# The LayerNorm's Newton step of the first stage from VectorE to GpSimd, and its normalised rows one row block per step

## The chip, the cores and the metric

The kernel runs on one core of a Trainium2 chip. The metric is the device time of one execution in microseconds; runs of one kernel are compared by their median. The profile is that of one profiled execution on the same core. PE is TensorE, DVE is VectorE, ACT is ScalarE, POOL is GpSimd, and SP is the engine whose queue issues most of the transfers.

## The reference

One decoder layer on x of shape (2, 2048, 512), that is 4096 rows of 512, in float32: a fixed-weight attention block, a cross attention over 128 context rows, and a mixture of 32 experts with a shared expert. The change touches the first block only:

```python
def _layernorm(x, axis=-1, eps=1e-05):
    m = jnp.mean(x, axis=axis, keepdims=True)
    v = jnp.var(x, axis=axis, keepdims=True)
    return (x - m) / jnp.sqrt(v + eps)

def attn(residual):                    # residual = _layernorm(x)
    x = _layernorm_gb(residual, ln_g, ln_b)   # the same again, with gain and bias
    q = x.reshape(Bx, Tx, 4, 128).transpose(0, 2, 1, 3)
    k = w_fc.reshape(-1, 128)          # 2048 keys
    v = w_proj.T.reshape(-1, 128)
    p = jnp.square(jax.nn.relu(jnp.einsum('bhtd,sd->bhts', q, k)))
    out = jnp.einsum('bhts,sd->bhtd', p, v)
    return residual + merged_heads(out)

x = x + attn(_layernorm(x))            # first stage
x = x + cross_attention(_layernorm(x), ctx, mask)
x = x + mixture_of_experts(_layernorm(x))
```

Both LayerNorms in a row need two reciprocal square roots of the same variance: with v the variance of a row, 1/sqrt(v + eps) for the residual, and 1/sqrt(v(1 + eps) + eps^2), the two in one, for the rows that go into the attention. The kernel computes them together as eight columns for the four row blocks of a tile.

## The kernel before

The work is one program of four parts: the first stage (`stage0`), the cross attention (`stage1`), the shared expert with the routing (`shared`), and the experts (`routed`). All matrix products are split: a float32 operand is written as a high and a low part (`split`, L89 to L97: the high part by a cast on ACT or DVE, the low part by a subtraction on DVE or POOL), and three matmuls make one product.

`stage0` handles 8 tiles of 512 rows. Its main loop runs over `steps`, (tile t, head h, key block kt): 8 x 4 x 16 = 512 steps. A step makes one 128x512 score tile `s` with three matmuls (L349) in one of four PSUM banks (P1 and P2, two each, by the parity of kt), lets ACT take the relu `rl` (L353) and DVE multiply `s` by it (L357, the square), splits the result into `ph` and `pl` (for five steps of eight, those with the result in SBUF, `pl` is made by POOL, for the other three by DVE), and multiplies `ph`, `pl` with the values (`av`, L311) seven steps later (LAG = 7).

Between these steps the next tile is prepared by the generator `prep(t + 1)`: at kt = 2 of head 0 it loads four row blocks `xt` (L238), and from kt = 7 on every odd kt calls it once. A call makes one part up to the next `yield`:

- four times `bn_stats` and `bn_aggr` of a row block on DVE (L243, L244), one call each
- `ve` (L247, L248) on DVE, the power -0.5 on POOL (`power`, L249, into `ap`), and on DVE one Newton step of it (L250 to L252: `at`, `at`, `ar`) and the offsets `ao` = -mean * `ar` (L254)
- the normalised rows `y` of the four row blocks on ACT (L264), two per call
- `bv` = 1 + `ar` on DVE (L270), and on POOL the residual rows x + layernorm(x), in place in `xt` (L273), each stored to `x1` by SP (L274), two per call

Tile 0 is prepared ahead of the loop, with two of its rows made by DVE. `prep_head` (L278) later turns the rows `y` by transposes on PE (L281), applies gain and bias on ACT (`gb`, L282) and splits them into `qh` and `ql`. Another generator, `background`, does context and weight work in other steps (wk, wv, wq, wo, and the shared expert's sums); its loads and stores go through SP's queue too.

The order within each engine's queue isn't the program's order. A scheduler places the instructions by their priority and by a simulated timeline when the kernel is built. The queues then run in that order on the chip, each waiting on semaphores. The same pools of tiles are shared by all: `xt` has four buffers, `y` six.

Of the kernel before, what the change touches and what calls it, by code (L numbers as in the profile page):

```python
# [14 lines left out]
A = mybir.AluOpType  # L15
# [65 lines left out]
@contextmanager  # L81
def later(g, n):

    g.tc.cur_priority += n
    yield
    g.tc.cur_priority -= n


def split(g, hi, lo, src, lo_engine=None, hi_engine=None):  # L89

    if isinstance(lo_engine, cycle):
        lo_engine = next(lo_engine)
    if hi_engine is None:
        g.nc.scalar.copy(hi, src)  # L94
    else:
        hi_engine.tensor_copy(hi, src)
    g.low = (lo_engine or g.nc.vector).tensor_tensor(lo, src, f32(hi), A.subtract)  # L97
# [16 lines left out]
def weight_steps(g, dram, nk, width, name, lo_engine=None):  # L114
    hi, lo = ([[g.piece(name + z)[:] for _ in range(width // 512)] for _ in range(nk)] for z in "hl")
    yield from split_steps(g, dram, hi, lo, lo_engine)
    return hi, lo


def part(w, k, c):  # L120

    return w[k][c // 4][:, c % 4 * 128:c % 4 * 128 + 128]


def run(steps):

    try:
        while True:
            next(steps)
    except StopIteration as end:  # L130
        return end.value
# [31 lines left out]
def three(terms):  # L163

    (wh, wl), (xh, xl) = terms
    return (wl, xh), (wh, xl), (wh, xh)
# [55 lines left out]
def stage0(g, x, wfcT, wpT, lnT, x1, background, front):  # L222
    nc = g.nc
    NT = T // 512
    LAG = 7
    gb = g.c.tile([128, 2, 4], F32, name="gb")
    with later(g, 20):
        nc.sync.dma_start(gb[:], lnT)
    ys, qs = {}, {}

    def prep(t):

        rows = [slice(t * 512 + s * 128, t * 512 + s * 128 + 128) for s in range(4)]
        xt = [g.tile("G", "xt") for _ in rows]
        for v, r in zip(xt, rows):
            nc.sync.dma_start(v[:], x[r, :])  # L238
        yield
        mv = g.sm.tile([128, 4, 2], F32, name="am", tag="am")  # L240
        for i, v in enumerate(xt):
            s6 = g.small("as", 6)
            nc.vector.bn_stats(s6[:], v[:])  # L243
            nc.vector.bn_aggr(mv[:, i, :], s6[:])  # L244
            yield
        ve, r0, tt, rs, of = (g.small("a" + z, 8) for z in "vptro")
        nc.vector.tensor_scalar(ve[:, 0:4], mv[:, :, 1], EPS, None, A.add)  # L247
        nc.vector.tensor_scalar(ve[:, 4:8], mv[:, :, 1], 1.0 + EPS, EPS * EPS, A.mult, A.add)  # L248
        power = nc.gpsimd.tensor_tensor(r0[:], ve[:], g.mhalf[:], A.pow)  # L249
        nc.vector.scalar_tensor_tensor(tt[:], r0[:], -0.5, ve[:], A.mult, A.mult)  # L250
        nc.vector.tensor_tensor(tt[:], tt[:], r0[:], A.mult)
        nc.vector.scalar_tensor_tensor(rs[:], tt[:], 1.5, r0[:], A.add, A.mult)  # L252
        mean = mv[:, :, 0].unsqueeze(1).to_broadcast([128, 2, 4])
        nc.vector.scalar_tensor_tensor(of[:].rearrange("p (a n) -> p a n", a=2), mean, -1.0,  # L254
                                       rs[:].rearrange("p (a n) -> p a n", a=2), A.mult, A.mult)
        if t > 0:
            yield
        ys[t] = []
        for i, v in enumerate(xt):
            y = g.tile("C", "y")  # L260
            if t == 0 and i % 2:
                g.first = nc.vector.tensor_scalar(y[:], v[:], mv[:, i, 0:1], rs[:, 4 + i:5 + i], A.subtract, A.mult)
            else:
                nc.scalar.activation(y[:], v[:], AF.Identity, bias=of[:, 4 + i:5 + i], scale=rs[:, 4 + i:5 + i])  # L264
            ys[t].append(y)
            if i % 2:
                yield

        sc = g.small("bv", 4)
        nc.vector.tensor_scalar(sc[:], rs[:, 0:4], 1.0, None, A.add)  # L270
        for i, v in enumerate(xt):
            with g.after(power):
                nc.gpsimd.tensor_scalar(v[:], v[:], sc[:, i:i + 1], of[:, i:i + 1], A.mult, A.add)  # L273
            nc.sync.dma_start(x1[rows[i], :], v[:])  # L274
            if i % 2:
                yield

    def prep_head(t, h):  # L278
        pt = g.bank("P4", "pt")
        for s in range(4):  # L280
            nc.tensor.transpose(pt[:, s * 128:(s + 1) * 128], ys[t][s][:, h * 128:(h + 1) * 128], g.ident)  # L281
        g.q = nc.scalar.activation(pt[:], pt[:], AF.Identity, bias=gb[:, 1, h:h + 1], scale=gb[:, 0, h:h + 1])  # L282
        qh, ql = g.tile("E", "qh", FR), g.tile("F", "ql", FR)
        split(g, qh[:], ql[:], pt[:])
        qs[t, h] = (qh, ql)

    todo = prep(0)
    while 0 not in ys or len(ys[0]) < 4:
        next(todo)
    with g.after(g.first):  # L290
        kw = run(weight_steps(g, wfcT, 4, 512, "kw", cycle((nc.vector, nc.gpsimd))))
    low = g.low
    prep_head(0, 0)
    prep_head(0, 1)
    with g.after(g.q):
        vw = run(weight_steps(g, wpT, 4, 512, "vw"))
    with g.after(low):
        run(todo)
    prep_head(0, 2)
    prep_head(0, 3)  # L300

    P, oT, cur = {}, {}, {}

    def av(t, h, kt):
        p = P.pop((t, h, kt))
        if kt == 0:
            cur["o"] = g.bank("P3", "o")
        o = cur["o"]
        j, rb = divmod(kt, 4)
        for n, (w, y) in enumerate(three(([part(v, rb, j) for v in vw], p))):  # L310
            nc.tensor.matmul(o[:], w, y[:], start=kt == 0 and n == 0, stop=kt == 15 and n == 2)  # L311
        if kt < 15:
            return
        oT[h] = g.tile("D", "oT")
        nc.scalar.copy(oT[h][:], o[:])
        if h < 3:
            return
        for s in range(4):
            rows = x1[t * 512 + s * 128:t * 512 + s * 128 + 128, :]
            b = g.tile("IJ"[s % 2] if t < NT - 1 else "G", "b")  # L320
            nc.sync.dma_start(b[:], rows)
            pt = g.bank("P4", "pt")
            for hh in range(4):
                nc.tensor.transpose(pt[:, hh * 128:(hh + 1) * 128], oT[hh][:, s * 128:(s + 1) * 128], g.ident)
            nc.vector.tensor_tensor(b[:], pt[:], b[:], A.add)
            nc.sync.dma_start(rows, b[:])

    steps = [(t, h, kt) for t in range(NT) for h in range(4) for kt in range(16)]
    marks = []
    for i, (t, h, kt) in enumerate(steps):  # L330
        if h == 0 and kt == 2 and t + 1 < NT:
            todo = prep(t + 1)
            next(todo)
        if t + 1 == NT and h == 0 and kt == 14:
            todo = front
        if (t + 1 < NT and (h > 0 or kt > 6) or h > 0) and kt % 2:
            with g.after(*marks):
                next(todo, None)
        if (h > 0 if t > 0 else h > 1) and kt % 8 == 6 or t > 0 and h == 0 and kt == 14:
            with g.after(*marks):  # L340
                next(background, None)
        if h > 0 and t + 1 < NT and kt == 12:
            prep_head(t + 1, h - 1)
        if h == 0 and t > 0 and kt == 8:
            prep_head(t, 3)
        s = g.bank(("P1", "P2")[kt % 2], "s")
        j, rb = divmod(kt, 4)
        for n, (w, y) in enumerate(three(([part(k, j, rb) for k in kw], qs[t, h]))):
            nc.tensor.matmul(s[:], w, y[:], start=n == 0, stop=n == 2)  # L349
        if i >= LAG:  # L350
            av(*steps[i - LAG])
        r = g.tile("K", "rl")
        m0 = nc.scalar.activation(r[:], s[:], AF.Relu)  # L353

        apart = i % 8 in (1, 3, 5, 6, 7)
        p = g.tile("H", "p") if apart else s
        m1 = nc.vector.tensor_tensor(p[:], s[:], r[:], A.mult)  # L357
        marks = [m0, m1]
        ph, pl = g.tile("A", "ph", FR), g.tile("B", "pl", FR)
        split(g, ph[:], pl[:], p[:], nc.gpsimd if apart else None, nc.vector if i % 8 == 2 else None)  # L360
        P[t, h, kt] = (ph, pl)
    run(background)
    g.marks = marks
    for st in steps[len(steps) - LAG:]:
        av(*st)
# [1219 lines left out]
```

## Time and profile before

| | us |
|---|---|
| median of 3 runs | 2690.44 (2690.38 to 2690.57) |
| profiled execution | 2688.47 |
| its span, first to last instruction | 2686.7 |
| PE busy | 2631.5 (98%) |
| DVE busy | 2047.4 (76%) |
| ACT busy | 1873.9 (70%) |
| POOL busy | 1208.4 (45%) |
| mean granted TensorE clock | 0.997 |
| x1, the residual rows on POOL (L273) | 32 of 0.835 mean |
| the power on POOL (L249) | 8 of 1.646 mean |

The first column of a timeline row is the start in us from the span's start, the second the duration in us; then come the engine, the line, the operation, out<-in by the program's names, the shapes, the number of merged instructions, and in brackets the idle time of the engine just before and what released it. A row of a group has the number of instructions, the total busy us and the mean ns of one, and the idle time before them with its releasers. Line numbers are those of the kernel before.

### The profile page before, as it was taken

Reading aid. Unit: us, or ns where it says so; the run is one execution under the profiler, and the core shown is the slowest. Engines: PE = TensorE matmul, PEld = TensorE weight load, DVE = VectorE, ACT = ScalarE, POOL = GpSimd, SP = SyncE. Lnnn points to the kernel's source line nnn. Section 1 sums busy time; section 2 is a strip of 40 time slices with the busy share of each in tenths; the row PEclk is TensorE's granted clock in tenths of the full one; section 3 lists DMA queues with packets and bytes.
Section 4 is the critical chain, followed back from the end, with each engine's and each line's share of the span. In section 5 each row is a group of like instructions: output and inputs, shape, how many; then the busy total and the mean of one; then the engine's idle time right before and its main releaser. Section 6 shows DMA issues by size and latency. Waiting matters only on the chain. (4 is left out here: it accounts for less than half of the span.)

```text
span 2686.7 us, 47611 instructions
## 1 busy us (share of the span) xinstructions
PE 2631.5 (98%) x14593; PEld 2265.3 (84%) x14593; DVE 2047.4 (76%) x4569; ACT 1873.9 (70%) x4155; POOL 1208.4 (45%) x972
## 2 busy tenths in 40 slices
PE   7999999999999999999999999999999999999998
PEld 5888877877789999999988877878989899888886
DVE  7777777777777888898876794663777777778985
ACT  7887787788778778887874332343666677777885
POOL 5765676777654444444446569420122212212221
PEclk9999999999999999999999999999999999999999
DMA  4112112223120323433259656663898899999994
GB/s 154 60 67 95 56 60 91 93 104 102 41 75 23 103 97 127 130 128 131 88 183 358 213 188 203 237 224 94 266 283 280 280 306 294 303 280 292 330 323 139
DMA packets 282289, 463.72 MB, mean 173 GB/s; under 512 B 34512, under 2 KB 85712, under 8 KB 282032
## 3 DMA queue, kind: packets, MB, share of 16 engines
q1 hardware_dynamic: 267344, 433.50, 47.3%
q0 software_dynamic: 14688, 27.17, 4.8%
q8 instruction: 115, 1.88, 0.3%
q14 instruction: 142, 1.16, 0.1%
HBM read 359.58 MB, written 102.93 MB: 172 GB/s over the span
## 5 line engine op out<-in xcount | busy, mean ns | idle before, releaser
L97 DVE TENSOR_TENSOR rl<-raw,rh 128x512 fp32r<-128x512 f32 x768 | 488.0, 684 | 82.5 <-ACT rh L94 63.1
L94 ACT CAST rh<-raw 128x512 fp32r<-128x512 f32 x768 | 438.7, 621 | 130.0 <-DMA raw<-in_rg 87.2
L97 POOL TENSOR_TENSOR pl<-p,ph 128x512 fp32r<-128x512 f32 x320 | 411.1, 1297 | 232.8 <-ACT ph L94 199.2
L353 ACT ACTIVATE rl<-s 128x512 f32<-128x512 f32 x512 | 294.1, 605 | 43.3 <-PE s L349 36.5
L1356 POOL DMA_INDIRECT out_dram<-v,idx x46 | 112.8, 2452 | 462.1 <-ACT v L1354 377.9
L526 POOL TENSOR_TENSOR e<-e,ri 128x512 f32<-128x512 f32 x128 | 134.0, 1052 | 289.8 <-DVE ri L524 145.3
L357 DVE TENSOR_TENSOR p<-s,rl 128x512 f32<-128x512 f32 x320 | 215.2, 683 | 45.2 <-ACT rl L353 38.8
L94 ACT CAST ph<-p 128x512 fp32r<-128x512 f32 x320 | 199.9, 629 | 53.3 <-DVE p L357 51.3
L523 ACT ACTIVATE e<-e,mn 128x128 f32<-128x128 f32 x512 | 199.7, 392 | 25.1 <-DVE mn L518 23.7
L349 PE MATMUL s<-qh,kwl 128*128 128x512 f32 x512 | 206.1, 404 | 10.0 <-DVE p L357 6.4
L1019 PE MATMUL gu<-z,swh 128*128 128x512 f32 x672 | 209.5, 391 | 0.2 <-DMA z<-zT 0.2
L357 DVE TENSOR_TENSOR s<-s,rl 128x512 f32<-128x512 f32 x192 | 133.5, 695 | 98.4 <-ACT rl L353 97.9
L311 PE MATMUL o<-pl,vwh 128*128 128x512 f32 x512 | 203.1, 397 | 1.2 <-POOL pl L97 1.2
L311 PE MATMUL o<-ph,vwl 128*128 128x512 f32 x512 | 200.4, 393 | 0.7 <-ACT ph L94 0.7
L349 PE MATMUL s<-ql,kwh 128*128 128x512 f32 x512 | 200.1, 391 | 0.0
L349 PE MATMUL s<-qh,kwh 128*128 128x512 f32 x512 | 200.0, 391 | 0.0
L311 PE MATMUL o<-ph,vwh 128*128 128x512 f32 x512 | 199.7, 390 | 0.0
L496 PE MATMUL q<-yh,wql 128*128 128x256 f32 x512 | 147.3, 288 | 2.1 <-DVE v L556 2.1
L1019 PEld LDWEIGHTS gu<-z,swh 128*128 128x128 f32 x672 | 126.3, 188 | 26.5 <-DMA z<-zT 0.6
L496 PE MATMUL q<-yh,wqh 128*128 128x256 f32 x512 | 146.1, 285 | 0.0
L496 PE MATMUL q<-yl,wqh 128*128 128x256 f32 x512 | 145.9, 285 | 0.0
L97 DVE TENSOR_TENSOR pl<-s,ph 128x512 fp32r<-128x512 f32 x192 | 131.3, 684 | 16.9 <-ACT ph L94 13.9
(348 smaller groups left out, 7986.0 us busy)
## 6 DMA issues: line engine op xcount, KB each, us to landing
raw<-in_rg SPq DMA_DIRECT2D x256, 256.0 KB
raw<-in_ru SPq DMA_DIRECT2D x256, 256.0 KB
raw<-in_rd SPq DMA_DIRECT2D x256, 256.0 KB
z<-zT SPq DMA_DIRECT2D x112, 256.0 KB
raw<-in_sgu SPq DMA_DIRECT2D x48, 256.0 KB
swh<-wS SPq DMA_DIRECT2D x48, 256.0 KB
swl<-wS SPq DMA_DIRECT2D x48, 256.0 KB
xt<-in_x SPq DMA_DIRECT2D x32, 256.0 KB
```

The costliest lines, as they stand in the source:

```text
L94: g.nc.scalar.copy(hi, src)
L97: g.low = (lo_engine or g.nc.vector).tensor_tensor(lo, src, f32(hi), A.subtract)
L311: nc.tensor.matmul(o[:], w, y[:], start=kt == 0 and n == 0, stop=kt == 15 and n == 2)
L349: nc.tensor.matmul(s[:], w, y[:], start=n == 0, stop=n == 2)
L353: m0 = nc.scalar.activation(r[:], s[:], AF.Relu)
L357: m1 = nc.vector.tensor_tensor(p[:], s[:], r[:], A.mult)
L496: nc.tensor.matmul(o[:, i, :], part(w, k, p), y[k // 2][:, k % 2, :], start=n == 0, stop=n == 11)
L523: nc.scalar.activation(e[:, hs], e[:, hs], AF.Exp, bias=mn[:, h:h + 1], scale=-1.0, accum_out=su[:, h:h + 1])
L526: nc.gpsimd.tensor_tensor(e4, e4, ri[:].unsqueeze(2).to_broadcast([128, 4, 128]), A.mult)
L1019: nc.tensor.matmul(o[:], y, z, start=(at, x) not in begun, stop=j == 1 and m == 2, skip_group_check=True)
L1356: nc.gpsimd.indirect_dma_start(out=out, out_offset=bass.IndirectOffsetOnAxis(ap=idx[rows, b + j:b + j + 1], axis=0), in_=v[rows], in_offse ...
```

## The change

From tile 1 on, the Newton step, the offsets and `bv` are made by POOL instead of DVE. The five operations are written as eight: two products, a scaling with an addition, a product, two products for the offsets and their sign, and the addition for `bv`. One more `yield` stands behind them, and the normalised rows come one per call instead of two. Tile 0 stays as it was.

```diff
@@ prep(t) in stage0
         power = nc.gpsimd.tensor_tensor(r0[:], ve[:], g.mhalf[:], A.pow)
-        nc.vector.scalar_tensor_tensor(tt[:], r0[:], -0.5, ve[:], A.mult, A.mult)
-        nc.vector.tensor_tensor(tt[:], tt[:], r0[:], A.mult)
-        nc.vector.scalar_tensor_tensor(rs[:], tt[:], 1.5, r0[:], A.add, A.mult)
-        mean = mv[:, :, 0].unsqueeze(1).to_broadcast([128, 2, 4])
-        nc.vector.scalar_tensor_tensor(of[:].rearrange("p (a n) -> p a n", a=2), mean, -1.0,
-                                       rs[:].rearrange("p (a n) -> p a n", a=2), A.mult, A.mult)
-        if t > 0:
+        V = nc.vector if t == 0 else nc.gpsimd
+        if t == 0:
...
+        else:
+            V.tensor_tensor(tt[:], r0[:], r0[:], A.mult)
+            V.tensor_tensor(tt[:], tt[:], ve[:], A.mult)
+            V.tensor_scalar(tt[:], tt[:], -0.5, 1.5, A.mult, A.add)
+            V.tensor_tensor(rs[:], tt[:], r0[:], A.mult)
+            for a in range(2):
+                V.tensor_tensor(of[:, 4 * a:4 * a + 4], mv[:, :, 0], rs[:, 4 * a:4 * a + 4], A.mult)
+            V.tensor_scalar(of[:], of[:], -1.0, None, A.mult)
+            yield
             yield
         ys[t] = []
         for i, v in enumerate(xt):
...
             ys[t].append(y)
-            if i % 2:
+            if i % 2 or t > 0:
                 yield
 
         sc = g.small("bv", 4)
-        nc.vector.tensor_scalar(sc[:], rs[:, 0:4], 1.0, None, A.add)
+        V.tensor_scalar(sc[:], rs[:, 0:4], 1.0, None, A.add)
         for i, v in enumerate(xt):
```

In the changed kernel the lines from L250 on stand up to ten lines later: the new operations are L259 to L265, `bv` is L280, the rows `y` L274, the residual rows L283, the relu L363, the square L367.

More of the change, by code (lines that the diff above doesn't have):

```diff
@@ L249, in prep @@
         power = nc.gpsimd.tensor_tensor(r0[:], ve[:], g.mhalf[:], A.pow)
-        nc.vector.scalar_tensor_tensor(tt[:], r0[:], -0.5, ve[:], A.mult, A.mult)
-        nc.vector.tensor_tensor(tt[:], tt[:], r0[:], A.mult)
-        nc.vector.scalar_tensor_tensor(rs[:], tt[:], 1.5, r0[:], A.add, A.mult)
-        mean = mv[:, :, 0].unsqueeze(1).to_broadcast([128, 2, 4])
-        nc.vector.scalar_tensor_tensor(of[:].rearrange("p (a n) -> p a n", a=2), mean, -1.0,
-                                       rs[:].rearrange("p (a n) -> p a n", a=2), A.mult, A.mult)
-        if t > 0:
+        V = nc.vector if t == 0 else nc.gpsimd
+        if t == 0:
+            V.scalar_tensor_tensor(tt[:], r0[:], -0.5, ve[:], A.mult, A.mult)
+            V.tensor_tensor(tt[:], tt[:], r0[:], A.mult)
+            V.scalar_tensor_tensor(rs[:], tt[:], 1.5, r0[:], A.add, A.mult)
+            mean = mv[:, :, 0].unsqueeze(1).to_broadcast([128, 2, 4])
+            V.scalar_tensor_tensor(of[:].rearrange("p (a n) -> p a n", a=2), mean, -1.0,
+                                   rs[:].rearrange("p (a n) -> p a n", a=2), A.mult, A.mult)
+        else:
[7 more added lines that the diff above has]
+            yield
             yield
```

## The prediction

> **What bounds the kernel now.** I read the page first, then PE's timeline in the first stage, then DVE, ACT and POOL at the places where PE pauses, last the groups by form.
>
> ```profile
> span 2686.7 us, 47611 instructions
> PE 2631.5 (98%) x14593; PEld 2265.3 (84%) x14593; DVE 2047.4 (76%) x4569; ACT 1873.9 (70%) x4155; POOL 1208.4 (45%) x972
> ```
>
> PE is the bound. The first stage is a stream of 128x512 matmuls whose starts are 0.227 us apart, six per step (1.36 us). Only what interrupts that stream can be won. I went through PE's timeline from 40 to 690 us and added up what lies over 0.227 between one start and the next where it is over by 0.09 or more. All of it sits in seven places, at the preparations of tiles 1 to 7 (tile 0 is prepared before the loop): 2.8, 1.7, 1.7, 2.5, 2.5, 3.5 and 2.6 us, 17.3 in all. Between them no start is late by that much. So 17.3 us is the most that this change can bring. The largest pause of tile 4, on PE:
>
> ```profile
> 345.68 0.50 PE L311 MATMUL o<-ph,vwl 128*128 128x512 f32 x1
> 347.64 0.50 PE L349 MATMUL s<-qh,kwl 128*128 128x512 f32 x1 [1.46 <-DVE p L357]
> ```
>
> A score matmul waits for its bank, which DVE's squaring (L357) frees. Why DVE was late is seen on tile 3, in the timelines of POOL, DVE and ACT:
>
> ```profile
> 236.64 1.65 POOL L249 TENSOR_TENSOR ap<-av,mhalf 128x8 f32<-128x8 f32 x1 [1.58 <-DVE av L248]
> 238.26 2.55 POOL L97 TENSOR_TENSOR pl<-p,ph 128x512 fp32r<-128x512 f32 x2
> ...
> 238.33 1.25 DVE L250 SCALAR_TENSOR_TENSOR at<-ap,av 128x8 f32<-128x8 f32 x1 [0.84 <-POOL ap L249]
> 239.61 0.70 DVE L357 TENSOR_TENSOR s<-s,rl 128x512 f32<-128x512 f32 x1
> 240.22 0.61 DVE L251 TENSOR_TENSOR at<-at,ap 128x8 f32<-128x8 f32 x1
> ...
> 240.34 0.59 ACT L94 CAST ph<-s 128x512 fp32r<-128x512 f32 x1 [1.42 <-DVE s L357]
> ...
> 242.53 2.92 ACT L264 ACTIVATE y<-xt,ao,ar 128x512 f32<-128x512 f32 x4
> ```
>
> Three costs stand there. DVE, whose queue is in order, stops 0.84 us for the power. Its 128x8 operation then takes 1.25 us and ends as the first of POOL's two subtractions ends (238.26 + 1.3): a tiny operation on DVE waits for whatever POOL is running. And ACT does four normalised rows in one piece of 2.9 us, in which no score tile gets its relu. The groups (window 40 to 690) give the second cost its size:
>
> ```profile
> L270 DVE TENSOR_SCALAR bv<-ar 128x4 f32<-128x4 f32 x7 | 7.3, 1048 | 0.0
> L250 DVE SCALAR_TENSOR_TENSOR at<-ap,av 128x8 f32<-128x8 f32 x7 | 6.1, 865 | 2.1 <-POOL ap L249 2.0
> L251 DVE TENSOR_TENSOR at<-at,ap 128x8 f32<-128x8 f32 x7 | 5.5, 779 | 0.0
> L252 DVE SCALAR_TENSOR_TENSOR ar<-at,ap 128x8 f32<-128x8 f32 x7 | 3.8, 539 | 0.0
> L254 DVE SCALAR_TENSOR_TENSOR ao<-am,ar 128x8 f32<-128x8 f32 x7 | 1.1, 154 | 0.0
> ```
>
> In tile 0, where POOL is idle, the same five took 0.15 to 0.17 us each.
>
> **Removed.** Seven times five operations leave DVE: 7.3 + 6.1 + 5.5 + 3.8 + 1.1 = 23.8 us, and the 2.1 us of waiting for the power. DVE is busy 76%, so this is worth nothing by itself; it is worth the PE pauses that it causes. ACT's wait for ao in front of the rows (L264 idle 3.2 us in this stage, two tiles) goes as well, unless the new ao is late. Only the two additions and scalings that give ve (L247, L248) stay on DVE.
>
> **Added.** Eight operations per tile on POOL, 56 in all. No row has a 128x8 product on POOL. Bounds: 0.105 us (the MEMSET of mhalf, 128x8) and 0.70 us (the power on 128x2, L139). The nearest rows by kind are the subtractions on 128x256 (0.742) and 128x512 (1.297); the line through them gives 0.20 at 8 columns. Dependent ones follow each other with some 0.08 us between (L871 and L872: starts 1.38 apart, 1.30 long). I take 0.28. That is 2.2 us a tile on POOL, which in its timeline sits idle 3.0 to 5.9 us beside tiles 1, 3, 4 and 5, waiting for ACT. Behind the chain on POOL stand the subtractions pl. PE uses a pl up to seven steps (9.5 us) after its score, and the chain up to it (relu 0.61, square 0.68, cast 0.63, subtraction 1.30) takes 3.2 us and some waiting, so 2.2 us is covered; PE's own wait for pl is 1.2 us in the whole stage now. Were that cover gone, PE would stop one for one.
>
> **Moved.** The orders of both kernels differ in the first stage alone, so what is won there shifts the rest unchanged. ACT's rows come two to six, for tile 6 ten, relus later. In tile 1 they stand 3+1 and in tiles 2 to 5 2+1+1, with relus between; in tiles 6 and 7 still four in a row. POOL's residual rows (L273, 0.78 each) come three calls later and lie between subtractions instead of in one block of 3 us. Their stores on SP's queue move with them past a few stores of kst, vst and loads of weights. SP waits up to 26 us for these rows already, and the x1 rows are read back a tile (64 steps, 87 us) later: nothing. The transposes move with the rows; the first head is due more than 30 steps later: nothing.
>
> **What is left of the 17.3 us.** Four rows in a row, with no wait: tile 3 pauses 1.3 after them, tile 7 0.8, so 1.1 each for tiles 6 and 7: 2.2. Tile 1 (three in a row): 0.7. Tiles 2 to 5: 0.4 each, from tile 5, whose rows now stand 2+2 and where the pause behind the second pair is 0.2 to 0.4 at a time: 1.6. A pause of tile 2 at 131 us, ahead of the power: 0.4 stays. The seventh operation of the chain against ACT's turn: in tile 3 the chain may start when the subtraction of step 145 ends (243.5) and takes 7 x 0.28 = 2.0, so ao at 245.5; ACT's turn comes two relus later than now, 242.53 + 2 x 1.36 = 245.3. So some tiles wait a few tenths: 1.5 over all. Sum 6.4; won 17.3 - 6.4 = 10.9 us.
>
> The profiled execution took 2688.47 us (2686.7 of span and 1.8 around it), 1.97 under the median of 2690.44. 2688.47 - 10.9 = 2677.6, on the median's footing 2679.5 us.
>
> **Rivals.**
>
> *ACT is the limit there (no change).* From relu 84 to 96 of tile 2 PE needs 12 x 1.36 = 16.3 us. ACT, by the spacing of its rows, needs 12 x 0.945 for relu and cast, 4 x 0.71 for the rows, 2 x 1.17 for the two heads: 16.5, without the copy of oT (0.47) and the context's casts. If spreading doesn't help, each tile keeps some 2 us, 14 in all: 3 won, 2687 us. For it: heads now follow two relus behind the rows. Against it: pairs of heads elsewhere (steps 162 and 166) cost PE nothing, four banks cover them.
>
> *ao late (same).* At 0.70 us each, ao of tile 3 is ready at 248.4 and ACT waits 3.1. Tile 4 against tile 3 prices such a wait: 1.61 us of it, and 0.94 more pause, 0.58 for 1. So 1.8 + 0.4 for five tiles, 2.9 for two: 17, nothing won, 2690 us.
>
> *ao very late (slower).* The same path decides for slower when a tile loses over (17.3 + 5.4) / 7 = 3.2 us, which is at about 0.95 us for each small POOL operation. At 1.0: waits of 5.2, losses of 3.4 and 4.1 a tile, 25, so 8 worse: 2698 us. For it: the power, on the same shape, takes 1.64, and a 512-column subtraction 1.30. Against it: every row of POOL that isn't a power grows with its columns from about 0.2.
>
> *The step is only longer on POOL (slower).* Undisturbed, the five took 0.8 us on DVE in tile 0, the eight take 2.2: ao comes 1.5 us later. If DVE's waiting beside POOL cost PE nothing, the pauses would stay and 7 x 1.5 x 0.58 = 6 us come on top: 2696 us. Against it: on DVE beside POOL the five took 3.4 us a tile, not 0.8, and DVE's lateness is what PE's rows name. This is the way that the Trainium skill points to ("GPSIMD Engine Reference", section 4.1 Engine selection): ordinary elementwise work belongs on VectorE, since GPSIMD is about two times slower for operations with two inputs. The trace agrees for large tiles (a 128x512 subtraction takes 1.30 on POOL, 0.68 on DVE) and speaks against it for these small ones.
>
> **Numbers.** A measurement of this kernel can tell about 0.2%, 5.4 us, from no change. Forecast 0.70; ACT the limit 0.11; ao late 0.07; ao very late 0.07; longer on POOL 0.05. Faster 0.70, within 0.2% 0.18, slower 0.12. Range: all 17.3 won gives 2673; the upper end takes in both cases without change: 2692. What is left out is the two slower cases and a little at either end.
>
> **What would show it.** In the profile after: DVE without the five groups, and s<-s,rl in the preparations no longer behind a 128x8 operation; POOL's new rows at 0.2 to 0.35 us; L274 (the rows, now) waiting under 2 us in sum; PE's pauses at the seven places some 6 us in all. Wrong if POOL's small rows take over 0.7, if ACT waits for ao in most tiles, if PE waits for pl, or if the pauses stay with ACT full throughout.

## The result and the profile after

The changed kernel takes 2678.19 us (median of 6 runs, 2676.27 to 2678.86) against 2690.41 us for the kernel before (2688.37 to 2695.22): 12.2 us less, a ratio of 0.9952 with a 95% interval of 0.9941 to 0.9962. In a later batch on one chip it was 2677.84 against 2689.84.

The page after:

```profile
span 2677.0 us, 47634 instructions
PE 2627.2 (98%) x14593; PEld 2266.3 (85%) x14593; DVE 2028.8 (76%) x4534; ACT 1872.5 (70%) x4155; POOL 1217.7 (45%) x1028
```

DVE lost 35 instructions and 18.6 us, POOL took 56 more and 9.3 us. No engine's share moved by a point. The difference lies in when things happen. The timeline at the preparation of tile 3, POOL first, then DVE, then ACT (start, duration, engine, line, out<-in, idle time before):

```profile
234.16 2.56 POOL L97 TENSOR_TENSOR pl<-p,ph 128x512 fp32r<-128x512 f32 x2
236.69 0.20 POOL L259 TENSOR_TENSOR at<-ap 128x8 f32<-128x8 f32 x1
...
238.21 0.21 POOL L260 TENSOR_TENSOR at<-at,av 128x8 f32<-128x8 f32 x1
238.51 0.20 POOL L261 TENSOR_SCALAR at<-at 128x8 f32<-128x8 f32 x1
238.80 0.20 POOL L262 TENSOR_TENSOR ar<-at,ap 128x8 f32<-128x8 f32 x1
...
239.61 0.24 POOL L265 TENSOR_SCALAR ao<-ao 128x8 f32<-128x8 f32 x1
...
235.91 0.69 DVE L97 TENSOR_TENSOR pl<-s,ph 128x512 fp32r<-128x512 f32 x1
236.52 0.69 DVE L367 TENSOR_TENSOR s<-s,rl 128x512 f32<-128x512 f32 x1
...
240.98 1.53 ACT L274 ACTIVATE y<-xt,ao,ar 128x512 f32<-128x512 f32 x2
...
244.31 0.81 ACT L274 ACTIVATE y<-xt,ao,ar 128x512 f32<-128x512 f32 x1
...
246.65 0.81 ACT L274 ACTIVATE y<-xt,ao,ar 128x512 f32<-128x512 f32 x1
```

DVE goes from one large operation to the next while POOL subtracts, without the 1.25 us operation that stood there. A small product on POOL lasts 0.20 us, and three dependent ones start 0.29 apart. `ao` is ready at 239.85, 1.1 us ahead of ACT's first row, and the rows leave room for relus and casts between them. The groups (window 40 to 690) show the sizes:

```profile
L260 POOL TENSOR_TENSOR at<-at,av 128x8 f32<-128x8 f32 x7 | 1.4, 202 | 0.1
L280 POOL TENSOR_SCALAR bv<-ar 128x4 f32<-128x4 f32 x7 | 1.7, 242 | 0.0
...
L274 ACT ACTIVATE y<-xt,ao,ar 128x512 f32<-128x512 f32 x28 | 21.8, 823 | 0.5 <-POOL ao L265 0.5
```

ACT waits for the new `ao` 0.5 us in the whole stage. PE waits for the square on DVE three times, before it was seven times (us in total, times, longest; first the kernel before, then the changed one):

```profile
PE s L349 <- DVE p L357: 4.7, 7, 1.5
...
PE s L359 <- DVE p L367: 1.3, 3, 0.7
```

Two measures of the first stage serve below, both from PE's timeline in one profiled execution. The **pauses** are what the prediction counted, over 0.227 us between starts, at the seven preparations. The **length** is the time from the first score matmul to the last value matmul. It repeats to 0.1 us: 775.1 and 775.2 in two profiles of the kernel before, 760.9 twice for the changed kernel. The medians in the table are from several batches, in which the kernel before took 2689.8 to 2691.2.

| | pauses, tiles 1 to 7, us | sum | length | median |
|---|---|---|---|---|
| before | 2.9, 1.7, 1.7, 2.5, 2.5, 3.5, 2.6 | 17.4 | 775.1 | 2690.4 |
| changed | 0.7, 0.6, 1.0, 0.8, 0.3, 1.5, 0.6 | 5.5 | 760.9 | 2678.2 |
| e1_newton_only | 1.5, 0.3, 1.1, 1.2, 1.3, 1.5, 0.8 | 7.6 | 763.9 | 2681.3 |
| e2_rows_only | 1.2, 1.4, 0.7, 1.2, 1.1, 1.4, 1.6 | 8.7 | 767.8 | 2683.2 |
| e4_dve_later | 1.3, 1.0, 1.4, 1.3, 0.1, 1.4, 1.6 | 8.2 | 766.6 | 2683.3 |
| e3_three_more | 1.3, 0.6, 0.0, 0.2, 0.8, 1.2, 1.8 | 5.9 | 764.0 | 2681.7 |
| e8_three_more_dve | 5.2, 1.4, 2.1, 4.5, 2.9, 5.7, 4.1 | 25.8 | 787.8 | 2703.7 |
| e5_two_rows_pool | 0.7, 0.6, 0.2, 0.5, 0.0, 0.6, 0.3 | 2.9 | 759.2 | 2677.1 |
| e6_ve_pool | 0.0, 0.6, 0.8, 0.8, 0.1, 0.7, 1.8 | 4.7 | 761.0 | 2678.3 |
| e9_both | 0.0, 0.1, 0.2, 0.0, 0.1, 0.5, 0.4 | 1.3 | 758.0 | 2673.3 |

### The profile page after: what moved, and what is told of

Its sections match the earlier page's. It is cut to its first block, busy times and chain, and to the rows that moved or that the text cites. A ratio compares the mean times of both kernels' runs of the same rounds, so it can differ in the third digit from the quotient of the medians.

```text
span 2677.0 us, 47634 instructions
## 1 busy us (share of the span) xinstructions
PE 2627.2 (98%) x14593; PEld 2266.3 (85%) x14593; DVE 2028.8 (76%) x4534; ACT 1872.5 (70%) x4155; POOL 1217.7 (45%) x1028
## 5 line engine op out<-in xcount | busy, mean ns | idle before, releaser
L363 ACT ACTIVATE rl<-s 128x512 f32<-128x512 f32 x512 | 295.1, 605 | 44.1 <-PE s L359 39.2
L367 DVE TENSOR_TENSOR p<-s,rl 128x512 f32<-128x512 f32 x320 | 215.9, 684 | 52.2 <-ACT rl L363 43.0
L367 DVE TENSOR_TENSOR s<-s,rl 128x512 f32<-128x512 f32 x192 | 133.5, 695 | 94.5 <-ACT rl L363 94.4
```

## The experiments

**The Newton step on POOL alone: e1_newton_only**

```diff
 (changed kernel)
             V.tensor_scalar(of[:], of[:], -1.0, None, A.mult)
-            yield
             yield
...
-            if i % 2 or t > 0:
+            if i % 2:
                 yield
```

> The changed kernel, but the normalised rows come two per call with one yield ahead of them, as before; ACT's order has them four in a row in every tile. Theory A (two causes of like size: tiny DVE operations beside POOL, and four rows in one block on ACT): the pauses that DVE makes, some 7 us of the 17.3, go and some 1.1 us per tile stay behind the blocks: some 8 won, 2682 us. Theory B (DVE's operations are nearly all of it): as the changed kernel, 2678 us. Theory C (the later and spread rows are nearly all of it): 2690 us, no change.

Measured: 2681.33 us against 2691.21, ratio 0.9957 (0.9943 to 0.9971), length 763.9. Theory C falls: 9.9 us were won, where theory A expected 8. Theory B's 2678 lies inside the interval; against B speaks the length, 3.0 us over the changed kernel's. With the waiting beside POOL went two other things, the 2.1 us that DVE stopped for the power and 2.7 of the 3.2 us that ACT waited for `ao`; this run doesn't tell the three apart. What stays are blocks of rows. ACT and PE in tile 3:

```profile
240.88 2.94 ACT L273 ACTIVATE y<-xt,ao,ar 128x512 f32<-128x512 f32 x4
243.72 0.57 ACT L94 CAST ph<-s 128x512 fp32r<-128x512 f32 x1
...
244.34 0.49 PE L320 MATMUL o<-ph,vwl 128*128 128x512 f32 x1
245.07 0.50 PE L358 MATMUL s<-qh,kwl 128*128 128x512 f32 x1 [0.23 <-DVE pl L97]
```

The cast of a score tile comes behind four rows, DVE's subtraction waits for it, and PE for the bank that this subtraction frees.

**The later, single rows alone: e2_rows_only**

```diff
 (kernel before)
         if t > 0:
+            yield
             yield
...
-            if i % 2:
+            if i % 2 or t > 0:
                 yield
```

> The kernel before with the second yield and one row per call; the Newton step stays on DVE; ACT's order has single rows with relus between. Theory A: the pauses behind the blocks go, those that DVE makes stay: some 6 won, 2684 us. Theory B: 2689 to 2690 us. Theory C: 2678 us.

Measured: 2683.22 us, ratio 0.9969 (0.9958 to 0.9980), length 767.8. Theory A again (2684); theory B, by which the rows' order brings nothing, falls. ACT's wait for `ao` is that of the kernel before, and so are DVE's groups but for L248 (1.1 us there, 2.2 here) and `bv`, which took 7.3 us there and takes 2.7 here:

```profile
L250 DVE SCALAR_TENSOR_TENSOR at<-ap,av 128x8 f32<-128x8 f32 x7 | 6.0, 863 | 2.1 <-POOL ap L249 2.0
L251 DVE TENSOR_TENSOR at<-at,ap 128x8 f32<-128x8 f32 x7 | 5.4, 778 | 0.0
L252 DVE SCALAR_TENSOR_TENSOR ar<-at,ap 128x8 f32<-128x8 f32 x7 | 3.8, 538 | 0.0
...
L271 DVE TENSOR_SCALAR bv<-ar 128x4 f32<-128x4 f32 x7 | 2.7, 388 | 0.0
...
L265 ACT ACTIVATE y<-xt,ao,ar 128x512 f32<-128x512 f32 x28 | 22.8, 823 | 3.2 <-DVE ao L254 3.2
```

The parts don't add up. By the lengths they win 11.2 and 7.3 us alone and 14.2 together. One reason is that this run is not the rows' part alone. The later `bv` takes 4.6 us off DVE that e1_newton_only takes off as well; at that run's price (9.9 us won for 23.8 on DVE, 0.42 for 1) it is worth some 2 of the 7.3 us, an estimate. And ACT's order spreads the rows further than the changed kernel does: singly in tiles 1 to 5, 2+1+1 in tiles 6 and 7, where the changed kernel has four in a row. A second reason is argued and not shown: both causes use up the same slack, the four score banks by which PE runs ahead, so once one cause is gone, the other alone may no longer empty them.

**Stop for the power, or waiting beside POOL: e4_dve_later**

```diff
 (e2_rows_only)
         power = nc.gpsimd.tensor_tensor(r0[:], ve[:], g.mhalf[:], A.pow)
+        if t > 0:
+            yield
         nc.vector.scalar_tensor_tensor(tt[:], r0[:], -0.5, ve[:], A.mult, A.mult)
...
         if t > 0:
-            yield
             yield
```

> As e2_rows_only, but the Newton step on DVE comes one call (two steps) after the power, so that DVE need not stop for the power; the operations still run beside POOL. If it is the waiting beside POOL (0.5 to 1.0 us for a 128x8 operation) that delays DVE: as e2_rows_only within 1 us, 2684 us, and the five rows on DVE still sum to some 20 us. If it is the stop for the power in DVE's queue: as the changed kernel, 2678 us.

Measured: 2683.28 us, ratio 0.9968 (0.9956 to 0.9980), 0.1 from e2_rows_only. DVE's first Newton operation waits 0.0 us for the power here and 2.1 there, and the five still take 17.8 us on DVE (19.0 there). That brings 1.2 us of length and nothing that the medians show, so the stop for the power alone doesn't make the difference to the changed kernel, which is 5.7 us shorter still. What the stop is worth stays open, because the edit also makes `ao` later. ACT waits for it twice as long as in e2_rows_only:

```profile
L266 ACT ACTIVATE y<-xt,ao,ar 128x512 f32<-128x512 f32 x28 | 22.8, 820 | 6.7 <-DVE ao L256 6.7
```

At the prediction's 0.58 for 1, these 3.5 us more would hide some 2 us of gain, an estimate.

That small operations on DVE wait beside POOL, the traces show operation by operation. Of the 49 that make `ve`, the Newton step, the offsets and `bv` in the kernel before, 27 last over 0.3 us, and every one of them ends 0.022 to 0.029 us after a POOL operation ends; none of the other 22 has a POOL operation running from before its start to beyond its end. `bn_aggr` (L244), with one input, isn't held: 10 of 28 have such a POOL operation over them and take some 0.17 us like the rest. The Trainium skill, "SBUF — State Buffer", section Who interferes with whom, states the rule: VectorE and GpSimd share a pair of SBUF ports as an exclusive lock held for a whole instruction; a VectorE instruction with two SBUF inputs contends for it with a GpSimd one that reads SBUF, and so does a VectorE instruction in a two-port mode, which a tensor_scalar can enter. These endings agree with the first half for the 18 that have two inputs, and so does the square, which reads one operand from PSUM and takes 0.67 to 0.70 us beside POOL and without it. The other 9 are tensor_scalars (6 of `bv`, 3 of `ve`) with one input; which mode they ran in, no run here shows.

**More work in the chain on POOL: e3_three_more**

```diff
 (changed kernel)
             V.tensor_tensor(rs[:], tt[:], r0[:], A.mult)
+            for _ in range(3):
+                V.tensor_tensor(tt[:], rs[:], rs[:], A.mult)
+                V.tensor_tensor(tt[:], tt[:], ve[:], A.mult)
+                V.tensor_scalar(tt[:], tt[:], -0.5, 1.5, A.mult, A.add)
+                V.tensor_tensor(rs[:], tt[:], rs[:], A.mult)
```

> The changed kernel with three more Newton steps on POOL (12 more small operations a tile in the chain to ao, 0.20 each and some 0.08 between dependent ones: 3.4 us). The scheduler puts the rows six to ten relus later and four in a row. If POOL's time is covered by its idle time and the seven steps of lag: only the blocks of rows cost, 2682 us, like e1_newton_only. If a longer chain on POOL goes to PE at 0.58 us for 1 (the price of ao late): 7 x 3.4 x 0.58 = 14 us more than the changed kernel, 2692 us.

Measured: 2681.70 us, ratio 0.9961 (0.9947 to 0.9974). Eighty-four more operations on POOL (17.0 us busy) cost PE nothing against e1_newton_only, which has the same blocks of rows but in tile 5 (3+1 here): 764.0 and 763.9 of length. ACT waits 0.0 us for `ao` here, since its order has the rows later, so the run tests the cover of POOL's time and not the price of a late `ao`. One of their groups, and PE's wait for POOL, which e1_newton_only has with 1.1 us:

```profile
L267 POOL TENSOR_TENSOR ar<-at,ar 128x8 f32<-128x8 f32 x21 | 4.3, 204 | 0.8
...
PE o L326 <- POOL pl L97: 0.9, 2, 0.5
```

**The same work on DVE: e8_three_more_dve**

```diff
 (kernel before)
         nc.vector.scalar_tensor_tensor(rs[:], tt[:], 1.5, r0[:], A.add, A.mult)
+        for _ in range(3 if t > 0 else 0):
+            nc.vector.scalar_tensor_tensor(tt[:], rs[:], -0.5, ve[:], A.mult, A.mult)
+            nc.vector.tensor_tensor(tt[:], tt[:], rs[:], A.mult)
+            nc.vector.scalar_tensor_tensor(rs[:], tt[:], 1.5, rs[:], A.add, A.mult)
```

> The kernel before with three more Newton steps on DVE: nine more 128x8 operations a tile, 63 in all; the counterpart of e3_three_more. Waiting beside POOL: each takes the 0.73 us that L250 to L252 took on average, 45 us more on DVE; e1_newton_only took 23.8 us of such operations off DVE and won 9.9, 0.42 us for 1, so some 19 us slower than before, 2710 us. If their length beside POOL didn't matter (0.15 each, 9.5 us): some 4 us slower, 2694 us.

Measured: 2703.65 us against 2690.57, ratio 1.0043 (1.0028 to 1.0058), length 787.8, 12.7 more than before. The size lies between the two expectations: the 63 operations took 24.8 us, 0.39 each, neither 0.73 nor 0.15. The timeline shows why, DVE and then POOL:

```profile
52.40 0.15 DVE L255 TENSOR_TENSOR at<-at,ar 128x8 f32<-128x8 f32 x1
52.58 0.17 DVE L256 SCALAR_TENSOR_TENSOR ar<-at,ar 128x8 f32<-128x8 f32 x1
52.66 0.69 DVE L97 TENSOR_TENSOR pl<-s,ph 128x512 fp32r<-128x512 f32 x1
53.27 1.26 DVE L254 SCALAR_TENSOR_TENSOR at<-ar,av 128x8 f32<-128x8 f32 x1
54.56 0.17 DVE L255 TENSOR_TENSOR at<-at,ar 128x8 f32<-128x8 f32 x1
...
50.55 1.30 POOL L97 TENSOR_TENSOR pl<-p,ph 128x512 fp32r<-128x512 f32 x1 [2.75 <-ACT ph L94]
53.21 1.29 POOL L97 TENSOR_TENSOR pl<-p,ph 128x512 fp32r<-128x512 f32 x1 [1.36 <-ACT ph L94]
```

The operation at 53.27 waits to POOL's end at 54.50; its successors run while POOL has nothing. POOL is idle there (2.75 and 1.36 us) for a cast on ACT, and each of these two casts had waited for DVE's square, 0.73 and 0.57 us: the late DVE has left POOL without work.

The run adds work and waiting together: at 0.15 each, 9.5 of the 24.8 us would be there without POOL. And tile by tile the loss doesn't follow the time of the operations. From the first score matmul of one tile to that of the next, the stretch in which tile 1 is prepared got 4.1 us longer, with 2.1 us more of small operations on DVE; that of tile 2 got 1.1 us shorter, with 3.0 us more. So the run shows that small operations are dear on DVE where three Newton steps on POOL were free (e3_three_more), but not the price of the waiting; why tile 2 gained is open.

**What follows the first stage: e7_before_again** (the kernel before, unedited)

> The kernel before, unchanged, for a second profile. In the profiles the first stage of the changed kernel is 14.2 us shorter, but what follows it takes 1899.6 us against 1895.6, though its orders are the same. If that is the spread of one execution: what follows takes 1898 to 1902 us here too. If it is given back for a reason: 1895 to 1896 us again.

Measured: 2694.09 us in its one execution. The first stage repeats (775.2), what follows took 1900.9 us against 1895.6 in the first profile. Over all profiles here, with the same orders after the first stage, it takes 1896 to 1903 us. So 4 us between two single profiles there is spread and not the change.

**Two rows on POOL, ve on POOL, and both: e5_two_rows_pool, e6_ve_pool, e9_both**

```diff
 (changed kernel)
-        nc.vector.tensor_scalar(ve[:, 0:4], mv[:, :, 1], EPS, None, A.add)
-        nc.vector.tensor_scalar(ve[:, 4:8], mv[:, :, 1], 1.0 + EPS, EPS * EPS, A.mult, A.add)
+        V = nc.vector if t == 0 else nc.gpsimd                      # e6, e9
+        V.tensor_scalar(ve[:, 0:4], mv[:, :, 1], EPS, None, A.add)
+        V.tensor_scalar(ve[:, 4:8], mv[:, :, 1], 1.0 + EPS, EPS * EPS, A.mult, A.add)
...
+            elif t > 0 and i % 2:                                   # e5, e9
+                nc.gpsimd.tensor_scalar(y[:], v[:], rs[:, 4 + i:5 + i], of[:, 4 + i:5 + i], A.mult, A.add)
             else:
                 nc.scalar.activation(y[:], v[:], AF.Identity, bias=of[:, 4 + i:5 + i], scale=rs[:, 4 + i:5 + i])
```

> The changed kernel, but two of the four normalised rows of tiles 1 to 7 are made on POOL (0.78 us each there). If blocks of rows on ACT are what is left of the pauses (5.5 us over the seven tiles in the changed kernel): some 3 us faster than the changed kernel, 2675 us. If POOL's queue becomes late in their place (six operations of 0.78 in a row ahead of the subtractions): as the changed kernel or up to 5 us slower, 2678 to 2683 us.

> The changed kernel with ve (L247, L248) on POOL as well, so that no tiny operation but bn_aggr stays on DVE. These two take 5.3 us in the seven tiles on DVE now, three of fourteen beside POOL; at 0.42 us for 1 some 2 us faster than the changed kernel, 2676 us; if the bound there is ACT's rows: no change, 2678 us.

Measured: e5_two_rows_pool 2677.07 us, ratio 0.9947 (0.9933 to 0.9960), length 759.2; e6_ve_pool 2678.26 us, ratio 0.9949 (0.9935 to 0.9963), length 761.0. Two rows less on ACT take half of the remaining pauses away, but 1.7 us of length and not the 3 expected. `ve` on POOL alone wins no length; it moves pauses from one tile to another, and the 2 us expected didn't come. The medians can't tell either from the changed kernel. Then both together, beside the changed kernel and e5 again on one chip (before 2689.84):

> e5_two_rows_pool and e6_ve_pool together. By the pauses of the first stage (5.5 us in the changed kernel, 2.9 with two rows on POOL, 4.7 with ve on POOL) some 2 us of pauses are left at best: 3 us faster than the changed kernel on the same chip. If two rows on POOL leave nothing for ve to gain, as e5_two_rows_pool within 1 us.

> The changed kernel, unchanged, beside the next two versions on one chip: 2677 to 2679 us, ratio 0.995, first stage 760 to 761 us.

> e5_two_rows_pool once more beside the changed kernel: first stage 759 us, 1.7 us under the changed kernel's; the whole 1 to 2 us under it, which this many runs may not tell apart, since what follows the first stage spreads over 5 us.

Measured: e9_both 2673.30 us (2671.12 to 2674.49), ratio 0.9936 (0.9922 to 0.9949); the changed kernel 2677.84 (2676.93 to 2680.06), 0.9956 (0.9942 to 0.9969), length 760.9; e5 again 2675.07, 0.9944 (0.9931 to 0.9958), length 759.1. e9_both is faster than both kernels: its slowest run lies under the changed kernel's fastest. By length it gains 2.9 us, as expected, by the medians 4.5. e5 again is 1.8 us shorter by length than the changed kernel. PE's waits between 40 and 690 us have come down to one line:

```profile
PE o L324 <- POOL pl L97: 0.4, 1, 0.4
```

## Why the prediction was right

2679.5 us were predicted and 2678.2 measured, 10.9 and 12.2 us won.

- *The bound.* That only PE's pauses at the seven preparations can be won holds. The count was a little small: it took the spacings behind score and value matmuls. By PE's timeline 11.6 of the 14.2 us of length went there, and 2.6 at the same preparations behind the transposes and the context's matmuls. So 17.3 was not quite the most: e9_both won 17.1 of length and has 1.3 of pauses left.
- *The cause.* Of the three costs that I named, the stop for the power, the waiting beside POOL and the rows in one block, the first two went with the Newton step (11.2 us of length alone, e1), and spreading the rows won as well (e2). The waiting is shown in the durations: the five took 23.8 us on DVE in the seven tiles, some 6 if undisturbed. That it, and not the stop for the power or ACT's wait for `ao`, makes most of the 11.2 us is likely and not shown: taking the stop away brought 1.2 us of length, but made `ao` later (e4). I hadn't set the costs against each other, and their gains don't add up (e1, e2).
- *POOL's operations.* 0.28 was taken with the hand-over, from a line through 256 and 512 columns; 0.29 was measured between dependent starts, 0.20 to 0.24 for one. The cover holds even for 17 us more (e3).
- *What is left.* 6.4 was the sum, 5.5 came: tiles 6 and 7 with their blocks 2.1 (2.2 predicted), tile 1 0.7 (0.7), tiles 2 to 5 2.7 (1.6, and 0.4 for the pause of tile 2). The term for `ao` being late, 1.5, was too large: ACT waits 0.5. Part of the error is made up by tiles 2 to 5, where more is left than was predicted.
- *The rivals.* ACT as the limit would have kept 14 us of pauses. It isn't the bound, but about half of what is left went with two of its rows (e5). For `ao` late, the price of small POOL operations decided, and it is a third of what that rival needed. For `ao` very late, my own sum gives 0.91 us for each operation and not 0.95, which changes nothing. That the step is only longer on POOL, with DVE's waiting free of cost, is refuted by e1: the step alone on POOL made the stage 11.2 us shorter, where this rival has it 6 longer.
- *One to one to the end.* Not settled to the last 2 us: the length fell by 14.2, the median by 12.2, and what follows spreads by 7 us from profile to profile. That 10.9 came so near to 12.2 is therefore in part luck: the count left out 2.6 us that the stage won, and 2.0 of what it won doesn't show in the medians.

## What to carry to other kernels

Look at the duration of the small operations, not only at their count: where a 128x8 operation takes 0.15 us in one place and 1.25 in another, compare its end with the ends on the neighbouring engine. A short serial chain that stands in the queue of an engine on PE's path may be better on a slower engine that has slack, even if it needs more instructions there. And the gains of two parts of a change needn't add up: try each alone, and look in the trace at what else the trial moved, here `bv`, the blocks of rows and the wait for `ao`.

## What the runs showed of the hardware

- A small operation on POOL costs 0.20 us (product, 8 columns) to 0.24 (addition, 4 columns), and 0.29 from start to start in a dependent chain. The power takes 1.67 for 8 columns, eight times the product on the same tile.
- A chain of small operations on DVE beside a busy POOL doesn't pay the wait each time: 0.39 us on average in e8 against 0.15 to 0.17 undisturbed. In the stretch shown, the late DVE also leaves POOL idle.
- In e8 two small DVE operations with two inputs ran beside a MEMSET of POOL, which reads nothing, in 0.15 and 0.17 us. It is a single MEMSET, but the one kind of POOL instruction that ran over such an operation from start to end and didn't hold it.
